# A graph kernel's block of 20 rows, moved from last to thirteenth

## The chip, the core and the metric

The kernel runs on one core of a Trainium2 chip. The metric is the device time of one execution in microseconds; lower is better. Five engines work side by side, each through its own queue in order: TensorE (PE, with its weight loads shown as PEld), VectorE (DVE), ScalarE (ACT), GpSimd (POOL) and SyncE (SP), which here only issues DMAs. [...]

## What is computed

Two layers over a graph of N = 2708 nodes with D = 256 features and a sparse adjacency matrix (about 0.3% filled, with a diagonal). Layer 0 is a plain graph layer; layer 1 adds attention in two steps. Cut to what matters:

```python
# layer 0
x = layernorm(x + relu(concat([x, adj @ x]) @ weight + bias))

# layer 1
R = adj + eye(N); R = R / R.sum(-1)
Z = 0; Xf = Xa = x
for n in range(2):
    logits = (Xa @ W1.T @ W2.T) @ (Xa @ W3.T).T
    A = softmax(logits), cut to each row's largest entries that make up 0.9, rescaled
    Xf = R @ Xf
    Xa = A @ Xa
    Z = Z + Xf @ U1[n].T + Xa @ U2[n].T
x = layernorm(x + layernorm(x + Z))
```

## The kernel before, in words

**Tiling.** The rows are cut into NB = 22 blocks of P = 128; the last one, EDGE = 21, has only 20 rows. Nothing is reordered by a planner: each engine's queue is the program order of the Python code.

**Layer 0** (L462 to L500) runs over the blocks in order. For block m TensorE multiplies the block's part of the adjacency with `y0` (L266, 44 matmuls; for the edge block L263, with 20 columns of weights, spread over four column groups whose sums `edge_sum` folds together, L250 and L254), adds the product of x itself (L477), and transposes the block before (`x1_transpose(m - 1)`, L453, copied by ScalarE in L454). After blocks 4, 8, 12, 16 and 20, `x1_qk` projects four finished blocks to queries and keys (L441, three copies each by ScalarE, L443 to L445). VectorE does the norm (L486 to L494, with one square root on ScalarE in L150). Two adjacency halves of 704 KB each are loaded for every block into a pool of three buffers (L235), so a block's second half can only be loaded when the first half of the block before has been read, by TensorE and by VectorE.

Accumulators `acc` are two PSUM buffers. The edge block's accumulator must be zeroed first (L182, on VectorE); before, that is asked for in block 20, after its norm.

**Lists of columns.** Beside the products, VectorE finds which columns of the adjacency are used: `name_columns` (L298 to L303) in every block, and from block ML = 16 on, `lists.take` (L330, L331), 20 rounds that pull out eight names each, spread over the blocks 16 to 21. `lists.end` then goes through GpSimd: store and reload (L343, L344), a short piece on VectorE (L348 to L350), seven scatters, each waiting for the one before (L354), and a reload (L357). The names of blocks 16 to 21 are turned by TensorE (L323) and handled in a second list, whose rounds and end lie in the first nine blocks of step 1.

**Between the layers** (L502 to L513) a tile `x1_edge` is made: GpSimd zeroes it (L508) and VectorE copies the edge block's 20 rows into it (L509); it is first read at the end of step 1's first block. Then the last transpose and the last x1_qk.

**Start of step 1** (L887 to L909). `begin1(t, n)` computes the logits of block t in three parts (L527; ScalarE copies each from the one PSUM tile `lg` to `es[t % 4]`, L534), with n projections by U1 after each part (`u1_project`, L670; copied by ScalarE, L673; stored by L674 and L675). `extract1(t)` on VectorE finds a block's 64 largest logits (L589 to L615, then L596 and L598), `exps1(t)` on ScalarE takes exponentials (L630, L632), `finish1(t)` on VectorE finds the threshold and masks (L646 to L659). It uses a tile `sums` whose first column GpSimd zeroes in L603. Quoted, since the order is the point:

```python
    begin1(0, 2)
    extract1(0)
    begin1(1, 2)
    part = exps1(0)
    part(0), part(1)
    begin1(2, 2)
    lists.take(0, 2)
    ra = finish1(0)
    extract1(1)
    part = exps1(1)
    part(0), part(1)
    for t in range(n_u, NB):
        u1_project(t)
    extract1(2)
```

**Step 1's loop** (L917 to L962): for block t TensorE transposes the masked weights in six groups (L554, copied by L556), multiplies them with x1 (L583), and computes the logits of block t + 3; ScalarE takes the exponentials of block t + 2; VectorE masks block t + 1 and extracts block t + 3, then adds up `za` (L722) from the product of L719. The same loop gathers adjacency rows through GpSimd (L376). Step 2 follows in a similar manner with a different search for the threshold, and nothing in it is touched.

Of the kernel before, what the change touches and what calls it, by code (L numbers as in the profile page):

```python
# [38 lines left out]
CAP = 160  # L39
ML = 16  # L40
CW, CC = 128, 7
AT = 96


# [17 lines left out]
def gnn_two_layer_kernel(ctx: ExitStack, tc: tile.TileContext, N, xT_d, x_d, adj_d, w0_d, b0_d,  # L62
# [30 lines left out]
    assert SEG * (NS - 1) + 8 <= N <= SEG * NS == SEG2 * NS2 and N >= SEG2 * (NS2 - 1) + 8  # L93
    assert SEG * NS - P == (NB - 1) * P - AT and AT + N - (NB - 1) * P <= P
    assert NB == 3 * KS + 1 and CW == P and CAP % 8 == 0 and N < NB * P
# [63 lines left out]
def fast_path(ctx, tc, c, flags, fint, xT_d, x_d, w0_d, b0_d, w1_d, w2_d, w3_d, u1_d, u2_d, g_d, b_d):  # L159
    nc = tc.nc  # L160
    N, D, DA, NB, DC, KH, CHS, rows = c.N, c.D, c.DA, c.NB, c.DC, c.KH, c.CHS, c.rows
    ident = c.ident
    adj_d, out_d, x1_d, za_d = c.adj_d, c.out_d, c.x1_d, c.za_d
# [12 lines left out]
    def ps_tr():  # L176
        return ps.tile([P, 4, P], FP, tag="tr", name="tr")

    def ps_acc(t=None):
        acc = ps.tile([P, CH], FP, tag="acc", name="acc")  # L180
        if t == NB - 1:
            nc.vector.memset(acc[:, :D + 1], 0.0)  # L182
        return acc
# [5 lines left out]
    es = [big.tile([P, NW], FP, tag=f"E{i}", name=f"e{i}") for i in range(4)]  # L189
# [28 lines left out]
    for u, u_d in ((c.u1, u1_d), (c.u2, u2_d)):  # L218
        for s in range(2):
            weights.append(lambda u=u, u_d=u_d, s=s: nc.scalar.dma_start(  # L220
                out=u[:, :, s, :], in_=u_d[s].rearrange("(c p) e -> p c e", p=P)))
# [6 lines left out]
    x1 = big.tile([P, NB, D], FP, tag="x1", name="x1")  # L228


    adj_of = {}

    def adj_load(m, h):
        a = adjp.tile([P, KH, P], FP, tag="adj", name="adj_t")
        nc.sync.dma_start(out=a, in_=adj_d[m, :, h * KH:(h + 1) * KH, :])  # L235
        adj_of.setdefault(m, []).append(a)
# [3 lines left out]
    EDGE = NB - 1  # L240
# [16 lines left out]
    def adj_product(acc, m, y, n, stop):  # L257
        p = rows(m)
        halves = adj_of.pop(m)
        for k in range(NB):  # L260
            if m == EDGE:
                o = EW * (k % 4)
                nc.tensor.matmul(acc[o:o + p, :n], lhsT=halves[k // KH][:, k % KH, :p], rhs=y[:, k, :n],  # L263
                                 start=k < 4, stop=k >= NB - 4)
                continue
            nc.tensor.matmul(acc[:p, :n], lhsT=halves[k // KH][:, k % KH, :p], rhs=y[:, k, :n],  # L266
                             start=k == 0, stop=stop and k == NB - 1)
# [28 lines left out]
    def name_columns(m):  # L296
        for h in range(2):
            nc.vector.tensor_reduce(some[:, h * KH:(h + 1) * KH], adj_of[m][h], AX.X, ALU.max,  # L298
                                    apply_absolute_value=True)
        nc.vector.tensor_scalar(some, some, 0.0, None, op0=ALU.not_equal)  # L300
        for a, b, o in ((0, m, 0), (m + 1, NB, -1)):
            if a < b:
                nc.vector.scalar_tensor_tensor(names[:, m, a + o:b + o], ramp[:, a:b], -float(m * P * NB),  # L303
                                               some[:, a:b], op0=ALU.add, op1=ALU.mult)
# [93 lines left out]
    for t in range(NB):  # L398
        p = rows(t)
# [30 lines left out]
    def qk_project(s, a, b, src):  # L430


        for c_, (ka, kb) in enumerate(KPS):
            lo, hi = max(a, ka), min(b, kb)
            if lo >= hi:
                continue
            n, i, h = hi - lo, c_ // 2, c_ % 2
            po = ps_misc()
            for j in range(DC):
                w = wqkq[:, j, 1 - h:3 - h].rearrange("p h a -> p (h a)")  # L440
                nc.tensor.matmul(po[:, :n], lhsT=w, rhs=src(j)[:, lo - a:hi - a], start=j == 0, stop=j == DC - 1)  # L441
            own, other = (slice(DA * g, DA * g + DA) for g in (h, 1 - h))
            nc.scalar.copy(q[other, lo:hi], po[other, :n])  # L443
            nc.scalar.copy(q[own, lo:hi], po[other, :n])
            nc.scalar.copy(keys[s][own, i, lo - ka:hi - ka], po[own, :n])  # L445
# [3 lines left out]
    def x1_transpose(t):  # L449
        p = rows(t)  # L450
        tr = ps_tr()
        for j in range(DC):
            nc.tensor.transpose(tr[:, j, :p], x1[:p, t, j * P:(j + 1) * P], ident[:p, :p])  # L453
        nc.scalar.copy(x1T[:, :, t * P:t * P + p], tr[:, :DC, :p])  # L454

    def x1_qk(i):
        a, b = CHS[i]
        qk_project(0, a, b, lambda j: x1T[:, j, a:b])

    CB = CH // P  # L460
    lists = Lists(0, ML, flags[:, NF - 4:NF - 2], first_room)
    for m in range(NB):  # L462
        p = rows(m)
        xt = work.tile([P, D], FP, tag="in", name="xt", bufs=3)
        nc.scalar.dma_start(out=xt[:p], in_=x_d[m * P:m * P + p, :])
        if weights and m:
            weights.pop(0)()
        acc = edge_acc if m == EDGE else ps_acc()
        name_columns(m)
        adj_product(acc, m, y0, D + 1, False)  # L470
        if m == EDGE:
            acc = edge_sum(acc, D + 1, False)
        if m + 1 < NB:
            adj_load(m + 1, 0)
            adj_load(m + 1, 1)
        for j in range(DC):
            nc.tensor.matmul(acc[:p, :D], lhsT=xT[:, j, m * P:m * P + p], rhs=w0[:, j, :],  # L477
                             start=False, stop=j == DC - 1)
        if m:
            x1_transpose(m - 1)  # L480
        if m == ML:
            lists.turn()
        if m >= CB and m % CB == 0:
            x1_qk(m // CB - 1)
        h = work.tile([P, D], FP, tag="mid", name="h")
        nc.vector.tensor_add(h[:p], acc[:p, :D], b0[:p])  # L486
        nc.vector.scalar_tensor_tensor(h[:p], h[:p], 0.0, xt[:p], op0=ALU.max, op1=ALU.add)
        nc.vector.tensor_scalar(rinv[:p, m:m + 1], acc[:p, D:D + 1], 1.0, None, op0=ALU.add)
        mv, sd = ln_stats(nc, small, c.eps, h, p)
        nc.vector.reciprocal(rinv[:p, m:m + 1], rinv[:p, m:m + 1])  # L490
        ln_apply(nc, x1[:p, m, :], h, p, mv, sd)
        nc.sync.dma_start(out=x1_d[m * P:m * P + p, :], in_=x1[:p, m, :])
        xb = work.tile([P, D], FP, tag="x1b", name="xb")
        nc.vector.tensor_add(xb[:p], x1[:p, m, :], c.gb[:p, 1, :])  # L494
        nc.sync.dma_start(out=c.x1b_d[m * P:m * P + p, :], in_=xb[:p])
        if m == EDGE - 1:
            edge_acc = ps_acc(EDGE)
        if m >= ML:
            i = m - ML
            lists.take(CAP // 8 * i // (NB - ML), CAP // 8 * (i + 1) // (NB - ML))  # L500
    assert not weights
    lists.end()  # L502
    y_room = big.tile([P, DC * N], FP, tag="Y", name="yg")
# [1 line left out]
    yg = y_room[:, :YW].rearrange("p (s c d) -> p s c d", s=2, d=D)  # L505
    spares = [y_room[:, YW + D * i:YW + D * (i + 1)] for i in range(4)]
    x1_edge = y_room[:, YW + 4 * D:YW + 5 * D]
    nc.gpsimd.memset(x1_edge, 0.0)  # L508
    nc.vector.tensor_copy(x1_edge[AT:AT + rows(EDGE)], x1[:rows(EDGE), EDGE, :])  # L509
    lists = Lists(ML, NB, flags[:, NF - 2:], yg[:, 1].rearrange("p c d -> p (c d)"))  # L510
    lists.turn()
    x1_transpose(NB - 1)
    x1_qk(len(CHS) - 1)  # L513

    NL = len(KPS) // 2

# [89 lines left out]
    def extract1(t):  # L606
        p = rows(t)
        e = es[t % 4]
        cand = small.tile([P, NS2 * 8], FP, tag="cand", name="cand", bufs=2)[:, :NS * 8]
        seg_max(cand, e, p, SEG, SEG)  # L610
        cv = cand.rearrange("p (s k) -> p s k", k=8)
        nmax = small.tile([P, 1], FP, tag="nmax", name="nmax", bufs=3)
        nc.vector.tensor_reduce(nmax[:p], cv[:p, :, 0], AX.X, ALU.max, negate=True)
        srt = small.tile([P, TOP1 + 1], FP, tag="srt", name="srt", bufs=3)
        nc.vector.tensor_reduce(srt[:p, TOP1:], cv[:p, :, 7], AX.X, ALU.max)  # L615
        put_in_order(srt, TOP1, cand, p)
        st1[t] = (nmax, srt)
# [48 lines left out]
    def u1_project(t):  # L666
        p = rows(t)
        pz = ps_acc()
        for j in range(DC):
            nc.tensor.matmul(pz[:p], lhsT=x1T[:, j, t * P:t * P + p],  # L670
                             rhs=c.u1[:, j].rearrange("p s e -> p (s e)"), start=j == 0, stop=j == DC - 1)
        o = v_out[:p, t % VS]
        nc.scalar.copy(o.rearrange("p s d -> p (s d)"), pz[:p])  # L673
        nc.sync.dma_start(out=c.yf_d[:p, t, :], in_=o[:, 1, :])  # L674
        nc.sync.dma_start(out=c.v_d[:p, t, :], in_=o[:, 0, :])  # L675
# [5 lines left out]
    def ya_pair():  # L681
# [15 lines left out]
        p = rows(t0 + 1)  # L697
        nc.scalar.copy(ya[AT:AT + p, t0 + 1, :], pz[:p, 1, :])

# [185 lines left out]
    n_u = 0  # L885

    def begin1(t, n):  # L887
        nonlocal n_u
        for i in range(NL):
            logits1(t, i)  # L890
            for _ in range(n):
                u1_project(n_u)
                n_u += 1

    nc.scalar.preload_act_table_set("natural_log_exp_and_others")
    begin1(0, 2)
    extract1(0)
# [9 lines left out]
    for t in range(n_u, NB):  # L907
        u1_project(t)
    extract1(2)  # L909
    ends = None  # L910

    at = {(m // 2, 3 * (m % 2) + 1): m for m in range(4)}
# [384 lines left out]
    for per in range(NB + 2):  # L1297
# [11 lines left out]
        for g in range(NG):  # L1309
            n = n_r * (g + 1) // NG - n_r * g // NG  # L1310
# [64 lines left out]
    n = len(new) + len(finals)  # L1375
# [381 lines left out]
```

## Time and profile before

| | us |
|---|---|
| median of 3 runs | 1281.5 |
| lowest, highest of them | 1278.85, 1284.95 |
| the profiled execution | 1286.8 |
| its span (first to last instruction) | 1284.9 |

| engine | busy us | share of the span |
|---|---|---|
| TensorE (PE) | 1202.1 | 94% |
| VectorE (DVE) | 973.9 | 76% |
| ScalarE (ACT) | 735.1 | 57% |
| GpSimd (POOL) | 634.9 | 49% |

The mean granted TensorE clock is 0.975. In the trace layer 0's first product starts at 28.7 us, its last (the edge block's) at 268.9; the first logits of step 1 are computed at 280.1, the loop of step 1 starts at 347.5 and step 2 shortly after 700.

A line of the timeline gives start, duration, engine, line, operation, result and operands, and in brackets the time for which the engine stood idle before it and what ended that. Waits sum such times by pair. The chain of waits is followed back from the last instruction; where it names one engine without a gap, that engine set the time.

### The profile page before, as it was taken

The numbers are of one execution on the slowest core, as the hardware profiler recorded it, in microseconds if no ns is written. First come the engines' busy times: TensorE is split into PE (matmuls) and PEld (weight loads), VectorE is DVE, ScalarE is ACT, GpSimd is POOL, SyncE is SP. The second block draws the span as 40 slices with busy tenths as digits, with TensorE's granted clock in tenths as the row PEclk, the third lists the DMA queues.
The fourth block names the chain that finished last, engine by engine and source line by source line (L and its number), as shares of the span: only waits on it lengthen the run. The fifth ranks groups of instructions, "written<-read, shape, count | busy, mean of one in ns | idle before, by whom it ended". The sixth has DMA issues, their size and how long they took to land.

```text
span 1284.9 us, 18709 instructions
## 1 busy us (share of the span) xinstructions
PE 1202.1 (94%) x5772; PEld 904.3 (70%) x5772; DVE 973.9 (76%) x3253; ACT 735.1 (57%) x1299; POOL 634.9 (49%) x597
## 2 busy tenths in 40 slices
PE   8999999987799999999999978999998999999885
PEld 6888888842377777777777646777766777776664
DVE  2455554973999998988871278979878999999886
ACT  2000111032566666666665498887888999989821
POOL 1000000004076552577766068878774878888860
PEclk9999999989899999999999888999999999999997
DMA  7455544523322220133334154665664555555451
GB/s 197 149 197 172 160 151 153 172 82 98 100 80 92 61 68 32 41 94 94 91 89 107 50 152 152 181 187 178 183 150 122 173 160 163 169 185 160 144 135 39
DMA packets 101703, 165.99 MB, mean 129 GB/s; under 512 B 17362, under 2 KB 74070, under 8 KB 101594
## 3 DMA queue, kind: packets, MB, share of 16 engines
q1 hardware_dynamic: 75308, 108.65, 26.1%
q0 software_dynamic: 20544, 51.17, 14.8%
q10 hardware_dynamic: 5742, 4.89, 1.3%
q8 instruction: 48, 0.79, 0.3%
q14 instruction: 61, 0.50, 0.1%
HBM read 130.74 MB, written 33.90 MB: 128 GB/s over the span
## 4 chain that ended last, share of the span: by engine, by line
PE 71%; DVE 10%; ACT 7%; DMA 6%; issue 3%; POOL 2%; SPq 0%; POOLq 0%; ACTq 0%; DVEq 0%
PE acc L583 23%; PE acc L266 16%; PE lg L527 8%; PE misc L769 6%; PE tr L554 6%; DMA yg<-yf_d,ix 3%; PE acc L670 2%; DMA yg<-v_d,ix 2%; DVE e L1110 2%; PE misc L402 2%; ACT e L988 2%; PE acc L691 2%; PE misc L441 2%; PE misc L719 2%; PE acc L477 1%
## 5 line engine op out<-in xcount | busy, mean ns | idle before, releaser
L556 ACT COPY wT<-tr 128x512 f32<-128x512 f32 (+2 forms) x258 | 136.6, 537 | 205.8 <-PE tr L554 205.8
L583 PE MATMUL acc<-ya,wT 128*128 128x256 f32 x924 | 223.1, 383 | 0.0
L739 POOL DMA_INDIRECT yg<-v_d,ix x154 | 193.5, 1256 | 59.3 <-issue 25.3
L583 PE MATMUL acc<-x,wT 128*128 128x256 f32 x882 | 217.4, 386 | 0.0
L739 POOL DMA_INDIRECT yg<-yf_d,ix x154 | 190.7, 1239 | 48.3 <-issue 26.2
L266 PE MATMUL acc<-y,adj_t 128*128 128x257 f32 x924 | 206.1, 382 | 0.0
L769 PE MATMUL misc<-yg,adj_t 128*128 128x256 f32 (+1 forms) x704 | 187.9, 398 | 18.1 <-DMA yg<-yf_d,ix 7.2
L583 PEld LDWEIGHTS acc<-x,wT 128*128 128x128 f32 x882 | 159.0, 190 | 58.1 <-issue 24.7
L583 PEld LDWEIGHTS acc<-ya,wT 128*128 128x128 f32 x924 | 172.1, 191 | 38.2 <-issue 16.7
L266 PEld LDWEIGHTS acc<-y,adj_t 128*128 128x128 f32 x924 | 174.9, 191 | 27.3 <-issue 1.9
L376 POOL DMA_INDIRECT adj_t<-in_adj,ix x154 | 168.4, 1094 | 50.9 <-issue 39.5
L769 PEld LDWEIGHTS misc<-yg,adj_t 128*128 128x128 f32 (+1 forms) x704 | 123.6, 191 | 69.6 <-issue 23.2
L527 PE MATMUL lg<-k,q 64*128 64x512 f32 (+3 forms) x528 | 138.0, 600 | 27.4 <-ACT e L534 13.5
L554 PE MATMUL tr<-ident,e 128*128 128x128 f32 (+1 forms) x946 | 145.2, 272 | 6.9 <-ACT wT L556 4.6
L554 PEld LDWEIGHTS tr<-ident,e 128*128 128x128 f32 (+1 forms) x946 | 117.7, 141 | 40.5 <-ACT wT L556 8.8
L343 POOL DMA_DIRECT2D part_d<-e x1 | 0.6, 573 | 278.6 <-DVE e L342 278.6
L988 ACT ACTIVATE e<-e,st 128x2708 f32<-128x2708 f32 (+1 forms) x43 | 113.5, 2640 | 0.1
L991 ACT ACTIVATE e<-e,st 128x2708 f32<-128x2708 f32 (+1 forms) x42 | 111.0, 2642 | 0.1
L454 ACT COPY x1T<-tr 128x256 f32<-128x256 f32 (+1 forms) x22 | 8.0, 365 | 179.8 <-PE tr L453 179.8
L589 DVE MAX8 cand<-e 128x8 f32<-128x170 f32 (+1 forms) x352 | 86.9, 318 | 15.9 <-ACT e L534 15.7
L1052 DVE MAX8 cand<-w 128x8 f32<-128x170 f32 (+1 forms) x352 | 94.1, 321 | 0.0
L527 PEld LDWEIGHTS lg<-k,q 64*128 64x128 f32 (+1 forms) x528 | 39.3, 183 | 59.1 <-issue 20.7
(246 smaller groups left out, 1749.6 us busy)
## 6 DMA issues: line engine op xcount, KB each, us to landing
adj_t<-in_adj SPq DMA_DIRECT2D x44, 704.0 KB
adj_t<-adjc_d SPq DMA_DIRECT2D x44, 448.0 KB
adjc_d<-adj_t SPq DMA_DIRECT2D x22, 256.0 KB
base<-za_d SPq DMA_DIRECT2D x40, 128.0 KB
adjc_d<-adj_t SPq DMA_DIRECT2D x22, 192.0 KB
xt<-in_x ACTq DMA_DIRECT2D x21, 128.0 KB
x_d<-x SPq DMA_DIRECT2D x21, 128.0 KB
x1b_d<-xb SPq DMA_DIRECT2D x21, 128.0 KB
```

The source lines that it names most:

```text
L266: nc.tensor.matmul(acc[:p, :n], lhsT=halves[k // KH][:, k % KH, :p], rhs=y[:, k, :n], start=k == 0, stop=stop and k == NB - 1)
L376: nc.gpsimd.indirect_dma_start(out=a[:CW, i, :], out_offset=None, in_=adj_rows, in_offset=bass.IndirectOffsetOnAxis(ap=ix[:CW, m, i:i + 1] ...
L527: nc.tensor.matmul(lg[:p, h, at:at + b - a], lhsT=q[o, t * P:t * P + p], rhs=keys[s][o, i, :b - a], start=True, stop=True)
L554: nc.tensor.transpose(tr[:, k % 4, :p], columns(e[:p], k), ident[:p, :p])
L556: nc.scalar.copy(wT[:, :len(ks), :p], tr[:, :len(ks), :p])
L583: nc.tensor.matmul(acc[:p, :D], lhsT=wT[:, k % 4, :p], rhs=part_y(y, k), start=k == 0, stop=k == NB - 1)
L589: nc.vector.max(dst[:p, i * 8:(i + 1) * 8], src[:p, i * step:i * step + w])
L739: nc.gpsimd.indirect_dma_start(out=y[:CW, i, :], out_offset=None, in_=rows_d, in_offset=bass.IndirectOffsetOnAxis(ap=ix[:CW, m, i:i + 1], ...
L769: nc.tensor.matmul(acc[:p, :D], lhsT=a[:kw, k, :p], rhs=y[:kw, k, :], start=k == 0, stop=k == CC)
L988: nc.scalar.activation(scr[:b.p, :N], e, AF.Relu, bias=b.nz, scale=b.l[k], accum_out=b.relu)
L991: nc.scalar.activation(scr[:b.p, :N], e, AF.Sign, bias=b.nz, scale=b.l[k], accum_out=b.sign)
L1052: nc.vector.max(b.cand[:p, 8 * i:8 * i + 8], low[:p, SEG2 * i:SEG2 * (i + 1)])
```

## The change

Four things change, all in layer 0 and at the start of step 1.

1. Layer 0's loop goes over blocks 0 to 11, then the edge block, then 12 to 20 (EARLY = 12). The edge block's adjacency is loaded once, in block 4, into free room of `es[2]`, with only the first 32 of the 128 columns of each piece. Its accumulator is asked for in block 11, before that block's norm.
2. The 20 rounds of `lists.take` are spread over five blocks instead of six.
3. Four `u1_project` calls come before the last transpose and the last x1_qk; `begin1` goes on with the fifth.
4. `x1_edge` is zeroed by VectorE, and both this and the copy come after `extract1(2)`.

```diff
+EARLY = 12
...
+    edge_a = es[2][:, :NB * 32].rearrange("p (k i) -> p k i", i=32)
+
     def adj_load(m, h):
+        if m == NB - 1:
+            if h == 0:
+                nc.sync.dma_start(out=edge_a, in_=adj_d[m, :, :, :32])
+                adj_of[m] = [edge_a[:, :KH], edge_a[:, KH:]]
+            return
         a = adjp.tile([P, KH, P], FP, tag="adj", name="adj_t")
...
-    for m in range(NB):
+    order = list(range(EARLY)) + [EDGE] + list(range(EARLY, EDGE))
+    for m, prev, then in zip(order, [None] + order, order[1:] + [None]):
...
         adj_product(acc, m, y0, D + 1, False)
+        if then == EDGE:
+            edge_acc = ps_acc(EDGE)
         if m == EDGE:
             acc = edge_sum(acc, D + 1, False)
-        if m + 1 < NB:
+        elif m + 1 < EDGE:
             adj_load(m + 1, 0)
             adj_load(m + 1, 1)
+        if m == CB:
+            adj_load(EDGE, 0)
...
-        if m:
-            x1_transpose(m - 1)
+        if prev is not None:
+            x1_transpose(prev)
...
-        if m >= CB and m % CB == 0:
+        if CB <= m < EDGE and m % CB == 0:
             x1_qk(m // CB - 1)
...
-        if m == EDGE - 1:
-            edge_acc = ps_acc(EDGE)
-        if m >= ML:
-            i = m - ML
-            lists.take(CAP // 8 * i // (NB - ML), CAP // 8 * (i + 1) // (NB - ML))
+        if ML <= m < EDGE:
+            i, n = m - ML, EDGE - ML
+            lists.take(CAP // 8 * i // n, CAP // 8 * (i + 1) // n)
...
-    nc.gpsimd.memset(x1_edge, 0.0)
-    nc.vector.tensor_copy(x1_edge[AT:AT + rows(EDGE)], x1[:rows(EDGE), EDGE, :])
     lists = Lists(ML, NB, flags[:, NF - 2:], yg[:, 1].rearrange("p c d -> p (c d)"))
     lists.turn()
-    x1_transpose(NB - 1)
-    x1_qk(len(CHS) - 1)
...
+    for n_u in range(4):
+        u1_project(n_u)
+    n_u = 4
+    x1_transpose(EDGE - 1)
+    x1_qk(len(CHS) - 1)
     nc.scalar.preload_act_table_set("natural_log_exp_and_others")
     begin1(0, 2)
...
     extract1(2)
+    nc.vector.memset(x1_edge, 0.0)
+    nc.vector.tensor_copy(x1_edge[AT:AT + rows(EDGE)], x1[:rows(EDGE), EDGE, :])
```

## The prediction

> **What bounds the kernel now.** I read the waits of TensorE and VectorE between 255 and 360 us (where the diff acts), then the chain of waits there, the timeline around each long wait, and short windows with the granted clock.
>
> TensorE's waits there (engine, line, who released it: us in total, times, longest):
>
> ```profile
> PE lg L527 <- ACT e L534: 13.5, 2, 13.0
> PE acc L263 <- issue: 3.4, 1, 3.4
> PE acc L670 <- ACT v_out L673: 2.4, 1, 2.4
> ```
>
> VectorE's, same stretch:
>
> ```profile
> DVE yg L509 <- POOL xs L603: 19.6, 1, 19.6
> DVE run L348 <- DMA e<-part_d: 5.9, 1, 5.9
> ```
>
> The 19.6 us is the root of the first and third TensorE wait. The timeline (start, duration, engine, line):
>
> ```profile
> 309.63 1.24 POOL L357 DMA_DIRECT2D ix<-list_d  x1 [1.41 <-DMA list_d<-e,to]
> 310.86 0.32 POOL L508 MEMSET yg<- 128x256 f32 x1
> 311.22 0.56 DVE L509 COPY yg<-x 20x256 f32<-20x256 f32 x1 [19.58 <-POOL xs L603]
> ```
>
> L509 copies into what L508 zeroes, so it waits for L508 (the view names L603, which ends in the same instant). L508 stands in GpSimd's queue behind the whole list chain (L343 at 285.60 to L357). Behind L509 on VectorE stand extract1(0), finish1(0), extract1(1); exps1 on ScalarE waits for these; and the lone `lg` PSUM tile waits for ScalarE. The chain of waits, 238 to 372:
>
> ```profile
> 263.75 1.74 PE misc L441 x8
> 265.50 3.41 issue
> 268.90 5.35 PE acc L263 x44
> ...
> 311.79 3.89 DVE cand L589 x16
> ...
> 342.11 5.46 PE acc L670 x8
> ...
> 350.33 1.13 PE lg L527 x4
> ...
> 362.78 0.44 PE tr L554 x4
> ```
>
> It is TensorE up to 265.5, then the edge block's own latency, later VectorE and ScalarE, and TensorE alone from 350.33. From 362.78 (block 1 of step 1) TensorE runs 16.90 us a block without a gap; VectorE, by the starts of L646 (364.18, 380.67, 397.18), needs 16.5. Windows (PE busy, then in the column before DMA the granted clock):
>
> ```profile
> 269.00:274.00 5.00, 5.00 (x44) 2.08 (x43) 4.83 (x11) 0.00 (x0) 0.00 (x0) 0.50 0.14 46
> 325.00:329.00 4.00, 3.67 (x6) 1.34 (x7) 3.83 (x9) 2.26 (x4) 0.00 (x0) 0.50 0.40 131
> 343.00:346.00 3.00, 3.00 (x4) 0.47 (x3) 2.69 (x14) 0.59 (x1) 0.00 (x0) 0.50 0.52 171
> ```
>
> After each of the three waits TensorE ran at half clock, the edge product (L263) included.
>
> **Part 1, the edge block thirteenth.** Removed at the end: 3.41 us of waiting for the zeroing of edge_acc (it sat behind block 20's norm), the 5.35 us product, and the latency from L250 to the start of L527 at 280.14. Added after block 11: the same work on a warm clock. The warm price of such 20-column matmuls is in the chain at 700 to 722:
>
> ```profile
> 715.87 0.56 PE acc L580 x8
> ```
>
> That is 70 ns each, so 44 x 70 = 3.1 us; with L250's copy 0.45, the fold 0.5, L477 0.88 and a transpose 0.22 it makes 5.2; I take 5.3 (bounds: 5.2, and 7.5 at the old clock). edge_acc's zeros now come in block 11, before its norm, and wait for nothing. x1_qk(4) then ends at 265.50 + 5.3 = 270.8.
>
> The new load: 128 x 22 = 2816 pieces of 128 bytes, 360 KB for 1408 KB. It stands on SP's queue behind block 5's loads (issued by 78.1) and before block 4's stores (88.74), needed ten blocks later. SP's issue grows from 0.33 us (128 pieces, L235) to 0.46 (256, L206): about 1 ns a piece, so 3 us. [...] By line rate (704 KB in 3.4 us, issue 251.7, over by 255.2) it lasts under 2 us; by the nearest small-piece row (L357, 2048 pieces of 28 bytes, landing in a median 4.0 us, on GpSimd's queue) about 5.5. Both fit the 10.6 us gap: cost 0. The edge block's other DMAs move with it: its x on ScalarE's queue and its two stores on SP's (0.3 us of issue each) stand before block 13's loads, where a block's stores always stand, some 3 us into the block before (133.89 and 134.79 for block 9), so they hold up nothing new. The old 1408 KB at the end no longer take part. name_columns of the edge block reads a quarter of the elements (3.13 us becomes about 0.9).
>
> **Part 2, candidates four per block.** The 20 rounds of take now fall on five blocks, four each (before: 3, 3, 4, 3, 3, 4). Four took 245.19 to 250.08 = 4.89 us, name_columns 3.54, the norm 2.91: 11.34 us a block against TensorE's 10.65. From the norm of block 16 (ends 224.31) the names of block 20 are done at 224.31 + 4.89 + 3.54 + 3 x 11.34 = 266.8, with the shift 272.1, while TensorE is free at 270.8: it waits 1.3 us for turn(). On the way block 20's second load is issued when VectorE has read block 19's first half, 253.5 in before's time; landing takes 3.4 to 3.6 (255.2; 261.8 to 265.4), TensorE wants it at 253.1 + 4.8 = 257.9. That holds with 0.8 to spare, and a stall up to 1.3 hides in the wait for turn().
>
> **Part 3, four projections ahead.** After turn (0.49): four U1 projections 4 x 1.82 = 7.3, transpose 0.22, a wait of about 0.8 for ScalarE's copy, x1_qk(5) 0.77. begin1(0) starts at 272.1 + 9.5 = 281.6, 1.5 later than the old 280.14, but four of the 22 projections are done. Their eight stores (L674, L675, 0.32 to 0.43 each) meet an SP queue that holds only block 20's two stores. Block 20's norm (x1 at 274.5) is covered entirely; were that cover gone it would cost about 2 us.
>
> **Part 4, the zeros on VectorE.** L508 goes and about 0.75 us (zeros and L509) stands behind extract1(2). VectorE is free of the list's end at about 287.5 (norm 275.0, four takes, then 1.26 and the 6.3 from L342 to L350), and es[0]'s last piece arrives at 291.0 + 1.5 = 292.5. extract1(0) ends near 299, takes near 301.5, not 324. What is late next: exps1(0) stands in ScalarE's queue behind begin1(1)'s copies, which ended at 308.34, now 309.8. It takes 3.2; finish1(0) starts at 313.1 against 324.41, so VectorE gains 11.3 and not 19.6. extract1(1) runs 317.8 to 327.1 (was 329.09 to 338.41), exps1(1) to 330.3, L556 and L534 1.6: the logits of L527 that stood at 350.33 come at 331.9, 18.4 us earlier. TensorE, out of projections at about 322.4, idles some 7.4 us before that.
>
> That idle costs clock. [...] The row is harsher: a wait of 2.4 us (339.7 to 342.1) already gave 0.50 for some 3.2 us, the 13 us wait for 3.7: 1.6 to 1.9. I take 1.9. By the same rows the waits of 1.3 and 0.8 us near 271 and 281 might cost up to 1.8; the 2 us at 277 left the clock at 1.00, so 0. Block 1 of step 1 starts at 346.2 (was 362.78): 16.5 earlier.
>
> **Afterwards.** VectorE now trails TensorE by 7.7 us (L646 353.9 against 346.2; before 1.4) and recovers 0.4 a block. At block 8 the second list's end holds it (L348 waited 4.62, L646 moved 6.3 further back); the lag reaches 4.9 + 6.2 = 11.1. `misc` must be freed by `za` (L722) before L719, 10.2 into a block: a wait of about 1.0, once (bounds 0 and 2.5). From block 9 there are no takes and the lag melts. From 708 on everything hangs on the same queues and shifts whole.
>
> Sum: 18.4 - 1.9 - 1.0 = 15.5. The profiled execution: 1286.8 - 15.5 = 1271.3; the median of the runs, 1281.5, stands 5.3 below it, so 1266.0.
>
> **The rivals.**
> (a) Full gain. If ScalarE and VectorE overlap better and the clock holds, the stall goes whole, 19.6 with the 3.4 of the edge less the 1.3 for turn: 21.7, so 1260. Against: exps1(0) stands behind begin1(1) in one queue. 8%.
> (b) GpSimd still holds VectorE. finish1(0) needs L603's zero column, also behind the list chain. The chain starts 4.2 earlier (281.4), L603 comes at 306.9, finish1(0) at 313.1. But VectorE now works beside it. [...] 11%.
> (c) Four takes starve the adjacency loads: if landing takes 5 us instead of 3.4 each of blocks 19 and 20 loses about 1.5, gain 12.5, time 1269. 12%.
> (d) No change: the waits move whole to ScalarE's queue, gain below 6.4. VectorE's 11.3 would have to be lost again; 7%.
> (e) Slower: the 128-byte load. If it lasts past 88.7 us it delays block 6's loads, wanted at 96.7. Beyond about 11 us each more us is lost; to eat 15.5 and 6.4 more it must last 33 us, 6 times my estimate, giving 1288 or more. 4%.
>
> **Numbers.** Main case 58%, its own range 1262 to 1270 (edge 5.2 to 7.5, clock 0 to 3.7, za 0 to 2.5). Over 0.5% (6.4 us, about what a measurement of this kernel can tell from no change) faster: 58 + 8 + 11 + 12 = 89; within: 7; slower: 4. Range 1259 to 1273, which holds the main case, (b), (c) and most of (a).
>
> **What would show it.** L509 without a wait for GpSimd; L263 at clock 1.0 in about 3.1 us near 163; L298 in blocks 16 to 20 trailing, but no new gap in L266; a short TensorE wait at L323; finish1(0) near 313; one TensorE gap of about 7 us near 324 to 332, then half clock; L527's next wait gone; step 1 in the same 16.90 us a block. I am wrong if exps1(0) doesn't follow begin1(1), if L266 shows gaps in blocks 5 to 7 or 17 to 20, or if step 1 gets longer per block.

## The result, and the profile after

| | before | after |
|---|---|---|
| median, us | 1282.33 | 1266.5 |
| lowest, highest | 1278.85, 1284.95 | 1263.92, 1267.37 |
| ratio, with 95% interval | | 0.9877 [0.9852, 0.9901] |
| profiled execution | 1286.8 | 1266.69 |
| its span | 1284.9 | 1264.8 |
| mean granted clock | 0.975 | 0.980 |

The changed kernel is 15.8 us faster by the medians; a median of 1266.0 was forecast, and all of its runs lie in the range. On the occasions of three later runs (warm6, after_again, exps_again) the kernel before itself took 1319 and 1328 us, so each kernel is compared only with the kernel before as measured beside it. Lines have moved down by 7 or 8, so L527 and L534 of before are L534 and L541 here, L646 is L653, L670 is L677.

TensorE's waits between 240 and 360 us (engine, line, who released it: us in total, times, longest):

```profile
PE lg L534 <- ACT e L541: 6.2, 1, 6.2
PE tr L331 <- DVE e L311: 0.8, 1, 0.8
PE misc L449 <- ACT x1T L462: 0.7, 1, 0.7
PE acc L274 <- DMA adj_t<-in_adj: 0.4, 1, 0.4
```

One long wait is left of the three, half as long, with a few short ones. VectorE's, same stretch:

```profile
DVE sc L653 <- ACT e L639: 11.5, 1, 11.5
DVE run L356 <- DMA e<-part_d: 5.0, 1, 5.0
DVE cand L596 <- ACT e L541: 2.6, 1, 2.6
...
```

VectorE no longer waits for GpSimd. What it waits for in its place is the exponentials on ScalarE (L639), and for 2.6 us a copy of the logits (L541). The timeline (start, duration, engine, line; in brackets the idle time before it and what ended that):

```profile
163.39 2.79 PE L271 MATMUL acc<-y,e 128*20 128x257 f32 x44
...
272.19 7.03 PE L677 MATMUL acc<-u,x1T 128*128 128x512 f32 x16
...
280.87 1.13 PE L534 MATMUL lg<-k,q 64*128 64x512 f32 x4
...
304.80 0.11 POOL L610 MEMSET xs<- 128x1 f32 x1
...
309.29 1.46 ACT L639 ACTIVATE e<-e,nmax 128x1408 f32<-128x1408 f32 x1
...
312.23 0.21 DVE L653 TENSOR_SCALAR sc<-z 128x1 f32<-128x1 f32 x1 [11.48 <-ACT e L639]
...
330.84 2.08 PE L534 MATMUL lg<-k,q 64*128 64x512 f32 x4 [6.21 <-ACT e L541]
...
344.61 0.60 PE L561 MATMUL tr<-ident,e 128*128 128x128 f32 x4
```

The edge product stands in mid-layer and takes 2.79 us; four projections fill TensorE from 272.19; step 1's first logits come at 280.87 (before 280.07); GpSimd writes its zero column at 304.80, over 4 us before ScalarE even starts the exponentials; finish1(0) begins at 312.23 (before 324.41); block 1 of step 1 begins at 344.61 (before 362.61; the 362.78 of the prediction is the same start in the chain of waits). The windows after the one long wait (PE busy first, the granted clock in the column before DMA):

```profile
330.00:332.00 2.00, 1.16 (x4) 0.51 (x4) 1.80 (x10) 1.28 (x2) 1.69 (x2) 0.50 0.25 66
332.00:334.00 2.00, 2.00 (x7) 0.97 (x4) 1.83 (x9) 1.01 (x1) 1.39 (x3) 0.51 0.13 37
```

Half clock again after the wait, until about 334; the edge product ran at 1.00 (163 to 166 us).

### The profile page after: what moved, and what is told of

Same layout as the page of the kernel before. It is cut to its first block, busy times and chain, and to the rows that moved or that the text cites. A ratio compares the mean times of both kernels' runs of the same rounds, so it can differ in the third digit from the quotient of the medians.

```text
span 1264.8 us, 18701 instructions
## 1 busy us (share of the span) xinstructions
PE 1195.3 (95%) x5772; PEld 904.6 (72%) x5772; DVE 971.3 (77%) x3254; ACT 735.0 (58%) x1299; POOL 632.6 (50%) x596
## 3 DMA queue, kind: packets, MB, share of 16 engines
q0 software_dynamic: 20544, 51.17, 15.4%
## 4 chain that ended last, share of the span: by engine, by line
PE 43%; DVE 7%; ACT 5%; DMA 4%; issue 1%; POOL 1%; POOLq 0%; ACTq 0%
PE acc L590 20%; PE misc L776 9%; PE lg L534 6%; PE tr L561 5%; DMA yg<-v_d,ix 3%; PE acc L698 2%; DMA yg<-yf_d,ix 1%; DVE e L1124 1%; PE misc L726 1%; ACT e L871 1%; DVE cand L1066 1%; DVE w L1119 1%; ACT e L1005 1%; ACT e L1002 1%; POOL yg L746 1%
## 5 line engine op out<-in xcount | busy, mean ns | idle before, releaser
L746 POOL DMA_INDIRECT yg<-yf_d,ix x154 | 186.9, 1214 | 48.3 <-issue 24.3
L384 POOL DMA_INDIRECT adj_t<-in_adj,ix x154 | 164.9, 1071 | 51.7 <-issue 40.3
L534 PE MATMUL lg<-k,q 64*128 64x512 f32 (+3 forms) x528 | 138.5, 602 | 19.4 <-ACT e L875 7.0
L534 PEld LDWEIGHTS lg<-k,q 64*128 64x128 f32 (+1 forms) x528 | 39.4, 184 | 51.4 <-issue 21.3
```

Source lines behind the costliest of these rows:

```text
L384: nc.gpsimd.indirect_dma_start(out=a[:CW, i, :], out_offset=None, in_=adj_rows, in_offset=bass.IndirectOffsetOnAxis(ap=ix[:CW, m, i:i + 1] ...
L534: nc.tensor.matmul(lg[:p, h, at:at + b - a], lhsT=q[o, t * P:t * P + p], rhs=keys[s][o, i, :b - a], start=True, stop=True)
L746: nc.gpsimd.indirect_dma_start(out=y[:CW, i, :], out_offset=None, in_=rows_d, in_offset=bass.IndirectOffsetOnAxis(ap=ix[:CW, m, i:i + 1], ...
```

## Experiments

All ratios are to the kernel before, measured beside each. The end of step 1 is the start of its edge product (705.2 before, 689.0 after, in one profiled run each). Layer 0 ends up to 1.6 us earlier or later from run to run, so starts are compared by their distance to something near, such as turn() (L331) in the kernels with part 1. From block 1 to the end of step 1 all traces here have the same 342.6 us, but for after (344.4) and exps_early (344.6), which wait once for `za`, and the three runs beside the slower kernel before (368 to 369). Step 2, the same code in all, took 575.8 to 581.2 us in the ten traces of the other occasions. So a single trace can be off by several us in its total, and the size of a part is taken from the medians.

**Part 4 undone: zeros_back.** The changed kernel with zeroing and copy at their old place.

```diff
     x1_edge = y_room[:, YW + 4 * D:YW + 5 * D]
+    nc.gpsimd.memset(x1_edge, 0.0)
+    nc.vector.tensor_copy(x1_edge[AT:AT + rows(EDGE)], x1[:rows(EDGE), EDGE, :])
...
     extract1(2)
-    nc.vector.memset(x1_edge, 0.0)
-    nc.vector.tensor_copy(x1_edge[AT:AT + rows(EDGE)], x1[:rows(EDGE), EDGE, :])
```

> The changed kernel with part 4 alone undone: zeros by GpSimd and the copy right behind them, as before. My theory (VectorE's wait for GpSimd's list chain is the root of the stall): the copy comes at about 305 (chain over at 304.8 in the changed kernel), extract1(0) runs 305.7 to 315.1, exps1(0) to 318.3, finish1(0) starts at 318.3 instead of 312.2, and everything from there is 6.1 later: 1272.6. Rival (the gain comes from the edge block's latency and cold product in layer 0, and VectorE's wait was harmless): within 1 of the changed kernel, 1266 to 1267.5.

Measured: 1273.01 (1272.21 to 1274.92), ratio 0.994 [0.9923, 0.9957]. Its timeline:

```profile
303.25 0.32 POOL L519 MEMSET yg<- 128x256 f32 x1
...
303.60 0.56 DVE L520 COPY yg<-x 20x256 f32<-20x256 f32 x1 [18.60 <-POOL xs L612]
...
335.41 2.08 PE L536 MATMUL lg<-k,q 64*128 64x512 f32 x4 [4.50 <-ACT e L543]
```

The wait for GpSimd is back with 18.6 us, and the second logits are at 335.41, 4.6 later than after, although this run's first logits came 1.3 earlier (279.6). That is 5.8 us by the trace. Block 1 starts at 350.77, which counted in the same way is 7.4 later: the half clock behind the wait lasted longer here (the eight matmuls of `acc` that follow the second logits took 3.78 us, 2.53 after). The medians give 6.5.

**Part 4 alone: zeros_only.** The opposite edit on the kernel before.

> The kernel before with part 4 alone: zeros and copy on VectorE behind extract1(2), nothing else changed. My theory: extract1(0) ends near 301, exps1(0) follows begin1(1) at 308.3, finish1(0) starts at 311.6 instead of 324.4, and the whole rest moves 12.8 forward: 1269.5. So most of the change's gain, without moving the edge block. Rival (layer 0 is what counts): at most 2 us of gain, 1280 or more.

Measured: 1271.52 (1268.52 to 1273.14), ratio 0.9915 [0.9897, 0.9933]. VectorE's longest wait is `DVE sc L644 <- ACT e L630` with 11.5 us, for ScalarE and not for GpSimd; finish1(0) starts at 312.8. Two lines, moved, bring 10 us, about two thirds of the whole. One of TensorE's waits is longer than before, though:

```profile
PE acc L668 <- ACT v_out L671: 4.2, 1, 4.2
```

This is the third of the three long waits (L670 there, 2.4 us), of which the prediction said that VectorE's 19.6 us were its root. With those gone it has grown, so it has a root of its own; no_u1_ahead below shows which.

**Parts 1 and 2 alone: edge_only.** The changed kernel without part 3 and with part 4 undone.

```diff
-    for n_u in range(4):
-        u1_project(n_u)
-    n_u = 4
     x1_transpose(EDGE - 1)
     x1_qk(len(CHS) - 1)
...
+    nc.gpsimd.memset(x1_edge, 0.0)
...
     extract1(2)
-    nc.vector.memset(x1_edge, 0.0)
```

(`n_u` then starts at 0, and the copy moves with the zeroing.)

> The changed kernel without parts 3 and 4: the edge block thirteenth and four rounds of take per block, but no projections ahead and the zeros on GpSimd. My theory: begin1(0) starts at 275.8 instead of 280.1 and the list chain, hence the copy and all behind it, comes 4.4 earlier: 1278. Rival (layer 0 is what counts): 10 us or more of gain, 1272 or less.

Measured: 1277.98 (1275.04 to 1281.8), ratio 0.9971 [0.9955, 0.9986]: 3.7 us. First logits at 275.5 instead of 280.1, and VectorE still waits 19.0 us for GpSimd. The two traces show a larger gain than the medians: block 1 starts at 353.8 instead of 362.6, 8.8 earlier. The one trace of the kernel before is a late one: its execution took 4.5 us more than the median, and its list chain (L343 to the end of L357) 25.3 us, where it takes 23.3 to 23.8 in this run, zeros_back, zeros_only, exps_early and the changed kernel. So the 3.7 of the medians is used, and why the rest of that trace is late stays open.

**Part 3 undone: no_u1_ahead.** The first half of the edit above, the zeros left on VectorE.

> The changed kernel without part 3: the last transpose and x1_qk come straight after turn(), and the four projections stay at the end of the start-up. My theory: begin1(0) starts near 275.8, exps1(0) follows begin1(1) near 304, finish1(0) starts at 307.3 (312.2 in the changed kernel), but then the last projections stand between exps1(1) and the loop again, so the loop's block 1 starts at 345.7 against 344.6: about 1267.5, i.e. part 3 is worth 1 us. Rival (the 7 us of projections that cover the norm are a gain of their own): about 7 slower than the changed kernel, 1273.

Measured: 1270.4 (1269.11 to 1272.0), ratio 0.9916 [0.9898, 0.9935]; between the two expectations and nearer to neither. My theory had counted part 3 as worth 1 us; by these medians it is worth 3.9. Counted from turn(), block 1 starts 3.9 us later than after, and step 1 ends 2.1 later, since this run has no wait for `za`. The timeline shows why:

```profile
323.00 1.45 ACT L639 ACTIVATE e<-e,nmax 128x1408 f32<-128x1408 f32 x1
...
325.81 1.04 ACT L680 COPY v_out<-acc 128x512 f32<-128x512 f32 x2
...
326.43 5.46 PE L677 MATMUL acc<-u,x1T 128*128 128x512 f32 x8 [4.21 <-ACT v_out L680]
...
334.64 1.13 PE L534 MATMUL lg<-k,q 64*128 64x512 f32 x4 [0.53 <-ACT e L541]
```

Four more projections than after are left when ScalarE turns to exps1(1). Their PSUM buffers are freed by ScalarE's copies (L680), which stand behind the exponentials, so TensorE waits 4.21 us, runs the last eight matmuls in 5.46 us instead of 3.70, and reaches the second logits at 334.64 instead of 330.84. Done ahead, these projections meet a free ScalarE.

The start is slower too. With nothing to do meanwhile TensorE waits 1.45 us for turn() and 2.03 for block 20's norm, and then runs at half clock (0.50 from 273 to 279 us):

```profile
272.83 0.66 PE L461 MATMUL tr<-ident,x 128*128 128x128 f32 x2 [2.03 <-DVE x L157]
...
275.24 2.08 PE L534 MATMUL lg<-k,q 64*128 64x512 f32 x4
277.25 4.88 PE L677 MATMUL acc<-u,x1T 128*128 128x512 f32 x8
```

In the changed kernel the same logits take 1.13 us, and eight matmuls of L677 are done in 3.70.

**Exponentials earlier: exps_early.** What is late next, by the timeline after, is ScalarE's order. Here exps1(0) stands after the first third of begin1(1), exps1(1) after the second third of begin1(2).

```diff
-    def begin1(t, n):
+    def begin1(t, n, later=None):
...
+            if later and i == later[1]:
+                part = exps1(later[0])
+                part(0), part(1)
...
-    begin1(1, 2)
-    part = exps1(0)
-    part(0), part(1)
-    begin1(2, 2)
+    begin1(1, 2, (0, 0))
     lists.take(0, 2)
     ra = finish1(0)
     extract1(1)
-    part = exps1(1)
-    part(0), part(1)
+    begin1(2, 2, (1, 1))
```

> The changed kernel with exps1(0) issued after the first third of begin1(1), and exps1(1) after the second third of begin1(2), instead of after them. My theory (after the change, ScalarE's queue order caps VectorE: finish1(0) waited 11.5 us for exps1(0)): finish1(0) near 303.3 instead of 312.2, TensorE's 6.2 us wait at L534 and the half clock behind it go, block 1 of step 1 starts near 337.7 instead of 344.6; VectorE's lag grows a little, so 1260. Rival (TensorE's own work bounds the start-up, the wait was slack): within 1 of the changed kernel.

Measured: 1261.7 (1258.52 to 1264.34), ratio 0.985 [0.9826, 0.9874]. TensorE's waits between 240 and 360:

```profile
PE tr L331 <- DVE e L311: 1.4, 1, 1.4
PE misc L449 <- ACT x1T L462: 0.7, 1, 0.7
PE lg L534 <- ACT e L541: 0.5, 1, 0.5
```

and VectorE's:

```profile
...
DVE cand L596 <- ACT e L541: 4.3, 2, 2.6
DVE sc L653 <- ACT e L639: 2.4, 1, 2.4
...
DVE qs L658 <- POOL xs L610: 0.6, 1, 0.6
```

The 6.2 us gap is gone, the 11.5 us wait is 2.4, and only now does GpSimd's zero column come last once, for 0.6 us. VectorE waits somewhat longer for copies of the logits (4.3 us instead of 2.6). Step 1 ends at 681.1, 7.9 earlier than after.

**Changed kernel and exps_early side by side: after_again, exps_again.** The two were measured together, beside a kernel before of 1328 us.

> The changed kernel itself, beside the next one on the same chip: 15 to 16 us under before, as measured.

> The changed kernel with the two earlier exponentials, on the same chip as the changed kernel itself: 4 to 8 us under it (4.8 by the medians of two separate measurements, 7.9 by the end of step 1 in the traces). If its earlier lead was only the scatter between measurements, within 2 us.

Measured: after_again 1315.83 (1312.84 to 1323.41), ratio 0.9906 [0.9874, 0.9938]; exps_again 1309.75 (1307.24 to 1310.5), ratio 0.985 [0.9809, 0.9891]. The earlier exponentials lead by 6.1 us, with no overlap of the two sets of times. Step 1's end differs by 8.0 (712.7 against 704.7), as in the first pair. The change itself brings 12.6 us by these medians, somewhat under the 15 to 16 expected; the interval takes both in.

**A clock kept warm: warm, warm6.** In the gap after the last projection TensorE does products whose result is not read, fourteen or six of them; everything else is the changed kernel.

```diff
+            if (t, g) == (0, 1):
+                fill = ps_misc()
+                for _ in range(6):
+                    nc.tensor.matmul(fill, lhsT=x1T[:, 0, :P], rhs=c.u1[:, 0].rearrange("p s e -> p (s e)"),
+                                     start=True, stop=True)
             if g < NL and t + 3 < NB:
                 logits1(t + 3, g)
```

> The changed kernel with 14 matmuls of 512 columns (some 6 us, into a tile that nobody reads) in TensorE's wait of 6.2 us before the second L534 of the loop. It adds work and takes nothing away. If that wait costs clock, as I say, L534 starts at the same 330.8 or a few tenths later but at clock 1.00, and block 1 starts 1.5 to 1.9 earlier than in the changed kernel. Rival (the slow rows behind the wait are not the clock but the work itself): no earlier, or later by what the filling overruns.

Measured: 1269.79 (1267.86 to 1271.13), ratio 0.9914 [0.9897, 0.9932]. The fourteen products took 12.2 us, twice what I had reckoned, and pushed the second logits to 335.37: as an experiment on the total it failed. But it ran at a clock of 1.00, and from the second logits to block 1 it took 12.3 us (335.37 to 347.66), where after takes 13.8.

> Six filler products instead of fourteen, which took twice the length I had reckoned (two records of 0.435 us each); six make 5.2 us and fit the gap of 6.2 us. The half clock is a real cost: the second logits start within 0.5 us of the changed kernel's distance behind the list's zero column, at a granted clock of 1.00, the stretch from them to the next group of products takes about 2.9 us instead of 4.4, and block 1 of step 1 comes 1.5 earlier in relation to them; the total is about 1265, too near to the changed kernel to tell apart. Rival (the half clock hides behind ScalarE and VectorE): the stretch shortens, block 1 does not come earlier.

Measured: 1307.68 (1295.82 to 1313.05), ratio 0.9875 [0.9784, 0.9966], too wide to use. Its windows answer:

```profile
328.00:330.00 2.00, 1.21 (x5) 0.46 (x6) 1.83 (x11) 1.26 (x3) 1.70 (x2) 1.00 0.24 66
330.00:332.00 2.00, 2.00 (x11) 1.74 (x12) 1.83 (x9) 0.98 (x1) 1.39 (x3) 1.00 0.14 37
```

The second logits start at 328.79, 18.6 us behind finish1(0), exactly the distance of after (330.84 less 312.23), at a clock of 1.00. From there to the next transposes it is 2.89 us (after: 4.38), to block 1 12.3 us, as in warm (after: 13.8). So the half clock costs 1.5 us after the change, and nothing hides it.

**The second list's end one block later: end_at_9.** After, block 9 shows one wait for `za` (L726, released by L729, 1.5 us), as forecast. Here `lists.end()` goes from block 8 to block 9.

```diff
-                if t == 8:
+                if t == 9:
```

> The changed kernel with the second list's end in block 9 instead of 8, where VectorE has no take any more. My theory (VectorE's wait for the list's store and reload, 4.6 us, on top of its lag, made TensorE wait 1.5 us once for za): that wait is gone, 1.5 earlier from there on. Rival (another wait takes its place): step 1 ends at the same time.

Measured: 1268.18 (1266.59 to 1269.61), ratio 0.9898 [0.9881, 0.9914]. TensorE's waits from 345 to 690, first after, then here:

```profile
...
PE misc L726 <- DVE za L729: 1.5, 1, 1.5
PE misc L726 <- ACT k L453: 0.5, 1, 0.5
```

```profile
...
PE misc L726 <- ACT k L453: 0.5, 1, 0.5
```

The row left out in each is the wait for the exponentials of step 2's first blocks (L875), near the end. The wait for `za` is gone, and from block 1 to the end of step 1 it is 342.6 us instead of 344.4: 1.8 shorter, as expected. In the total nothing can be seen of it: 12.0 us under the kernel before, where the changed kernel had 15.8 and 12.6 on its two occasions.

**Both edits: both.**

> The changed kernel with the earlier exponentials and the second list's end in block 9: the two sums together, 6.4 and 1.5 to 2, so 1258 to 1259. If one stall only hides the other, no better than the earlier exponentials alone.

Measured: 1261.23 (1256.93 to 1262.72), ratio 0.9851 [0.9835, 0.9868]: no gain over exps_early that these runs can tell.

## Why the prediction was right, point by point

| step | predicted | measured |
|---|---|---|
| edge product, warm | 3.1 us | 2.79 |
| whole edge block in mid-layer | 5.3 | 4.9 |
| wait for turn() | 1.3 | 0.8 |
| begin1(0) starts | 281.6 | 280.9 |
| GpSimd's zero column | 306.9 | 304.8 |
| finish1(0) starts | 313.1 | 312.2 |
| TensorE's gap before the second logits | 7.4 | 6.2 |
| the second logits | 331.9 | 330.8 |
| half clock after it | 1.9 | 1.5 |
| block 1 of step 1 | 346.2 | 344.6 |
| wait for `za` | 1.0 | 1.5 |
| end of step 1, earlier by | 15.5 | 16.2 |

The edge block's 4.9 is from its product's start (163.39) to block 12's product (168.33). The profiled span fell by 20.1, 16.2 of it by the end of step 1; the other 3.9 lie in step 2 (579.7 us before, 575.8 after), where the code is the same and the other eight traces of these occasions have 576.5 to 581.2.

**What is luck.** The steps came as forecast, most of them within some 1 us, and that is not luck. That the median came within 0.5 us is: the 16.2 rests on a late trace of the kernel before, the profiled execution itself was forecast at 1271.3 and took 1266.7, and measured again the change brought 12.6 us (by the interval 8 to 17) instead of 15.8.

**The root.** VectorE's copy behind GpSimd's list chain was the main cause, as said: taken away alone it brings 10.2 us, put back it costs 6.5. It was not the root of the third TensorE wait, as said above. And VectorE gained 12.2 us at finish1(0), not 19.6, because exps1(0) stands behind begin1(1)'s copies on ScalarE, also as said: moved forward, it gives another 5 to 6.

**The parts do not add up.** Against before, parts 1 and 2 bring 3.7 us; with part 4 11.3; with part 3 instead 8.7; with both about 15. So part 4 is worth 10.2 alone, 7.6 beside parts 1 and 2, 6.5 beside all; part 3 is worth 5.0 without part 4 and 3.9 with it. Each of these carries some 2 to 4 us of uncertainty by the intervals, and 6.5 and 3.9 the more, as the whole change was not measured beside these runs. That parts 3 and 4 gain shows in the traces too, at block 1; the last digits are not sure.

**What was mis-sized.** The largest is part 3. The prediction costed it as a delay of begin1(0) by 1.5 us with the norm as cover (about 2 us), and never said what would become of these four projections if they stayed: they would wait behind exps1(1). The row for it stood in its first list, L670 waiting 2.4 us for L673, and was put down to VectorE. The total came out right because it was worked out for the kernel with all its parts, where that wait does not arise; asked for the part alone (no_u1_ahead) I was off by 3 us. Of the 1.6 us by which block 1 came before its forecast, 1.1 stand at the second logits already (the chain over begin1(0) and finish1(0) ran about 1 us ahead throughout), and 0.4 is the clock; the rest is the difference of the two views.

**The clock.** In before a wait of 2.4 us was already followed by half clock (0.50 from 343 to 346 us); after, 6.2 us was (0.50 and 0.51 from 330 to 334). The waits of 0.8 us at 271 and of 0.7 at 280, which the prediction let cost up to 1.8, cost none: the granted clock is 1.00 in all windows from 270 to 284, and 280.87 runs the logits' four matmuls in 1.13 us. Its "0" for the 2 us at 277 holds for the kernel before only: no_u1_ahead's 1.45 and 2.03 us close together were followed by half clock. Nor is the price fixed: the 1.5 us after the change are 3.1 in zeros_back, where the stretch from the second logits to block 1 takes 15.4 us instead of 12.3. The prediction's 1.9, an estimate from some 3.7 us at half clock behind the 13 us wait of before, lies between the two.

**The rivals.** (b) fell: the zero column stood ready over 4 us before the exponentials began, since the seven scatters of the chain took 0.84 to 0.93 us each, as in zeros_back, where VectorE stood still beside them. That these scatters slow down beside VectorE, on which (b) rested, no run shows. (c) fell: four takes made one wait of 0.4 us for the adjacency. (d) fell: VectorE's wait did move to ScalarE's queue, but with 11.5 us in place of 19.6, and finish1(0) came 12.2 earlier. (e) fell: the issue of 2816 pieces took 0.66 us and not 3, the last of it was in at about 86 us, and block 6's loads were issued from 90.07; it was needed eight blocks after its issue, not ten as the prediction has it. (a) was not reached, but the way to it was the one named, ScalarE's queue.

**Left open.** Why step 2's length varies between 575.8 and 581.2 us was not looked into. Parts 1 and 2 were never taken apart. And part 4 changes two things, the engine that zeroes and the place in VectorE's queue; whether one of them would have done was not run.

## What to carry to other kernels

A small instruction that hands work to another engine is priced by what stands ahead of it in its own queue: two short lines behind GpSimd's chain of scatters cost 10 us, and moving them was worth more than moving a whole block of products. When such a wait is taken away, look in the next engine's queue for what was hidden behind it (here ScalarE's exponentials behind copies, worth another 5 to 6 us). And price a part by the kernel without it, not only by what it adds: projections that seemed only to fill a pause were worth about 4 us, because left for later they waited for PSUM buffers (4.21 us in no_u1_ahead).

## What the runs showed of the hardware

- A load of 2816 pieces of 128 bytes (352 KB, in the units of the 704 KB halves) was issued by SyncE in 0.66 us, and kept the DMA engines busy until about 86 us where they were idle from about 84 before: some 2 us more, about 7 us after its issue. Windows of the kernel before, then of the changed kernel (the last two columns are the DMA share and GB/s):

```profile
84.00:85.00 1.00, 0.92 (x2) 0.49 (x3) 0.96 (x5) 0.03 (x1) 0.00 (x0) 1.00 0.00 0
```

```profile
85.00:86.00 1.00, 1.00 (x4) 0.48 (x3) 0.43 (x3) 0.00 (x0) 0.00 (x0) 1.00 0.43 52
86.00:87.00 1.00, 1.00 (x6) 0.68 (x5) 0.00 (x0) 0.48 (x1) 0.00 (x0) 1.00 0.00 1
```

- The same edge product, in the same place at layer 0's end after the same wait of 3.4 us, took 5.35 us at clock 0.50 in the kernel before and 2.78 at 1.00 in zeros_only. The same holds for shorter ones: behind it before waited 1.95 us at L453 and kept 1.00 (first logits in 1.13 us), and zeros_only waited 2.00 and 1.87 us and fell to half clock (2.08 us). At these lengths a wait may or may not cost clock; one profile does not settle it.
- One gather's issue on GpSimd (L384, started at 313.70) took 3.76 us beside VectorE's L661 (313.61 to 316.64), and the six around it 0.94 to 1.01. In the kernel before one (L376, started at 366.70) took 2.62 beside L654 (365.47 to 368.50), and the four around it 0.94 to 1.05. In both the gather ended 0.82 us after VectorE's instruction; why, no run shows.
